# A GRU with routed experts on one core: a wait of VectorE moved to another bank, tanh ahead of z, a reordered head, more expert pieces in the search

## The chip, the cores and the metric

The kernel runs on one core of a Trainium2 chip. The metric is the device time of one execution in microseconds (us), lower is better. The kernel before takes 1180.23 us in the median of 3 runs (1180.09 to 1180.43).

## The reference, cut to what matters

A GRU runs over T = 256 steps of x (16 rows, 256 steps, 512 values); its states are the tokens of a routed layer with 16 experts that share one weight matrix. Each expert takes its 256 best tokens of 4096, and their weighted outputs are added to x.

```
def cell(h, x):
    gi = x @ W_ih + b_ih
    gh = h @ W_hh + b_hh
    i_r, i_z, i_n = jnp.split(gi, 3, axis=-1)
    h_r, h_z, h_n = jnp.split(gh, 3, axis=-1)
    r = jax.nn.sigmoid(i_r + h_r)
    z = jax.nn.sigmoid(i_z + h_z)
    n = jnp.tanh(i_n + r * h_n)
    h_new = (1.0 - z) * n + z * h
...
logits = xf @ router_w + router_b
S = jax.nn.softmax(logits, axis=-1)
G, idx = jax.lax.top_k(S.T, k)          # k = 256
out = jnp.einsum('ekh,hd->ekd', tokens, expert_w) + expert_b
y = jnp.zeros((bs, h)).at[idx.reshape(-1)].add((G[..., None] * out).reshape(-1, h))
return x + y
```

All work is in float32, except for the counts of the search.

## The kernel before, in words

**Stages.** There are four: a head that loads the weights and makes the input products of the first eight steps; the recurrence, 256 steps; the softmax over the experts; and a search for each expert's 256th largest weight, 15 bits of a float one after the other, then the gates, the rest of the expert products and the stores. The order of PE, ACT, DVE, POOL and (in the recurrence) SP is written out by hand: each engine gets its instructions in program order, and a wait on one holds everything behind it on the same engine.

**One step of the recurrence.** The state hs is kept with the 512 values in four blocks of 128 partitions. Each gate has an accumulator bank in PSUM (r, n and z), preset by ACT: r and z with the input products, n with the bias. In each bank the four 128-column blocks of the gate lie in quadrants of 32 partitions. Two steps share a bank: even steps write 16 rows of a quadrant, odd steps 32. A step is

- 96 matmuls on PE (L489, called by h_part): r and n of the first two blocks of hs, r and n of the second two, then z;
- on ACT the sigmoid of r (L579); in even steps the preset of the next r bank (L386) after it;
- on DVE a copy of one element, seen, from r (L583), then t = r * n for two halves (L630) and t + x part for two halves (L632);
- on ACT, for each half, tanh of t (L634) and then the sigmoid of z (L635), and after them presets and copies of the input products (L389, L396, L648 to L651);
- on DVE, by the list of calls, turn_n (L667, a transpose of t), turn_z (L670, of z), less_n (L673, u = h - n), by_z (L678, v = u * z) and plus_n (L681, the new hs), each for the halves 0 and 1. Every plus_n writes half of hs, of which the next step's first matmuls read the first.

In the same steps, after the h matmuls, PE also makes the input products for later steps (x_product, L462: seven products for four steps, in the manner of Strassen, from sums that DVE and ACT keep), router logits (L308) and the expert products of the first ten groups of 8 steps (L371); the number of pieces due is counted in `due`.

**Head.** The queues of SP and ACT carry the loads. Before, SP has the first x block, W_ih's rows 1 and 3 (k = 1, 3), W_hh's gate 2, the second x block (L261), expert weights, router weights, expert bias; ACT has W_ih's k = 0 and 2, W_hh's gates 0 and 1. PE transposes an x block (spread_x, L516), DVE copies it out (L519), PE makes the products of the first eight steps from it (x_part, L403, in four groups by k), and x_done (L414) adds the biases. The second block is transposed after all x_part; `spare` (L546) and `a_sum` (L545) are biases for the input sums, and x_sums makes the operands of the products from the second block. `keep_clock` and `begin_sums` (L90) are matmuls with zeros.

**Softmax and search.** 22 groups are late: their expert products are made from the last steps on, in units. expert_for(n) puts the next n units on PE; a unit is one k of a group for a quarter of the 512 columns (four matmuls of 128 columns, L110, one for each quadrant) until the gates exist, and for all columns after that. When a group is done, ACT copies its bank to ht (L148 to L150) and presets the bank of a following group with the expert bias (late_begin, L132). Four units stand in each of the last two steps, one in last_logits, six ahead of the softmax, five ahead of the search, six in each of its 15 bits, and 14 between the search and the gates. The softmax is the exp on ACT (L353, with a table load ahead of it), sums (L355), reciprocals (L357) and products (L360) on DVE; then PE transposes the weights (L832, L833), they are copied to sT, and each bit is a count on DVE (L760), a matmul that adds counts (L774), and two small operations (L777, L782) that give the next candidate.

Of the kernel before, what the change touches and what calls it, by code (L numbers as in the profile page):

```python
# [13 lines left out]
ALU = mybir.AluOpType  # L14
# [3 lines left out]
def kernel(  # L18
# [15 lines left out]
    nc = tc.nc  # L34
    B, T, D = x.shape
    E = router_w.shape[1]
    P = 128
    QD = 32
    KC = D // P
    TG = P // B  # L40
# [5 lines left out]
    xs = const.tile([P, NG, D], F32, name="xs")  # L46
    ht = const.tile([P, NG, KC, P], F32, name="ht")
    HD = D // 2
    ewr = const.tile([P, KC, E + D], F32, name="ewr")

    lg = const.tile([P, E, NG], F32, name="lg")
    eb = const.tile([P, D], F32, name="eb")
# [51 lines left out]
    ps_m = ctx.enter_context(tc.tile_pool(name="ps_m", bufs=2, space=bass.MemoryType.PSUM))  # L104
# [13 lines left out]
            )  # L118

    whole, halves_d = slice(0, D), [slice(0, HD), slice(HD, D)]  # L120
    quarters = [slice(P * i, P * (i + 1)) for i in range(KC)]

    late_items = [(g, whole) for g in late_groups[:-1]] + [(late_groups[-1], half) for half in halves_d]
    late = []
# [2 lines left out]
    gated = []  # L127

    def late_begin(pool):
        g, cols = late_items[len(late_done) + len(late)]  # L130
        pe = pool.tile([P, D], F32, name="pe", tag="pe")
        nc.scalar.copy(pe[:, cols], eb[:, cols])  # L132
        late.append(pe)

    def late_parts():
        for i, (g, cols) in enumerate(late_items):
            pe = late[0]
            for k in range(KC):

                for part in [cols] if gated or cols != whole else quarters:  # L140
                    late_part(g, pe, k, part)
                    if k == KC - 1 and part.stop == cols.stop:
                        if i + 2 < len(late_items):
                            late_begin(ps_m if (i + 2) % 6 < 2 else late_pool[0])
                        late.pop(0)
                        late_done.append((g, cols))
                        if gated:
                            late_sums[g, cols.start] = pe  # L148
                        else:
                            nc.scalar.copy(wide(g), pe)  # L150
                    yield

    late_pool = []
    parts = late_parts()

    def expert_for(n):
        for _ in range(n):
            next(parts, None)

    with (  # L160
        tc.tile_pool(name="wts", bufs=1) as wts,
# [8 lines left out]
        def slot(s):  # L170
            return 1 + (s - 1) % (2 * TG) if s else 0
# [67 lines left out]
        with tc.manual_schedule(engines={ET.SP, ET.Activation, ET.Pool}):  # L239
            def load_gate(gate, queue):  # L240
                queue.dma_start(
                    out=whh[:, :, gate, :],
                    in_=w_hh[:, gate * D : (gate + 1) * D].rearrange("(c p) n -> p c n", c=KC),
                )

            def load_k(k, queue):
                queue.dma_start(
                    out=wih[:, k].rearrange("p g d -> p (g d)"),
                    in_=w_ih.rearrange("(p c) n -> p c n", c=KC)[:, k, :],
                )  # L250

            nc.gpsimd.dma_start(out=c0, in_=cond)
            nc.sync.dma_start(out=xs[:, 0, :], in_=x[:, 0:TG, :])
            load_k(0, nc.scalar)
            load_k(1, nc.sync)
            load_k(2, nc.scalar)
            load_k(3, nc.sync)
            load_gate(0, nc.scalar)
            load_gate(2, nc.sync)
            load_gate(1, nc.scalar)  # L260
            nc.sync.dma_start(out=xs[:, 1, :], in_=x[:, TG : 2 * TG, :])  # L261
            nc.scalar.activation(dummy, ones[0:1, 0:1], AF.Sigmoid)
            for dst, src in (
                (b_raw[0:1], b_ih.rearrange("(o g d) -> o g d", o=1, d=D)),
                (b_raw[1:2], b_hh.rearrange("(o g d) -> o g d", o=1, d=D)),
                (b_n, b_hh[2 * D :].rearrange("(o d) -> o d", o=1)),
            ):
                nc.gpsimd.dma_start(out=dst, in_=src)
            nc.sync.dma_start(out=ewr[:, :, E:], in_=expert_w.rearrange("(c p) n -> p c n", c=KC))
            nc.sync.dma_start(out=ewr[:, :, 0:E], in_=router_w.rearrange("(c p) n -> p c n", c=KC))  # L270
            nc.gpsimd.dma_start(out=rb, in_=router_b.rearrange("(o e) -> o e", o=1).to_broadcast([P, E]))
            nc.sync.dma_start(out=eb, in_=expert_b.rearrange("(o d) -> o d", o=1).to_broadcast([P, D]))

        def biases(bank):
            for i, rows in enumerate((b_raw[:, 0, :], b_raw[:, 1, :], b_raw[0:1, 2, :], b_n)):
# [225 lines left out]
        def keep_clock(n, banks=idles):  # L501

            for i in range(n):
                begin_sums(banks[i % len(banks)])

        with tc.manual_schedule(engines={ET.PE, ET.Activation, ET.DVE, ET.Pool}):
            make_masks()
            for bank in banks:
                begin_sums(bank)
            keep_clock(8)  # L510
            held = (r_bank, n_bank, z_bank, x_bank0, x_bank1)

            def spread_x(g, bank):
                xT[g] = xtp.tile([P, TG // 2, P], F32, name="xt")
                for c in range(KC):
                    nc.tensor.transpose(bank[:, P * c : P * (c + 1)], xs[:, g, c::KC], ident)  # L516
                for q in range(TG // 2):
                    to = xT[g][:, q, :].rearrange("p (c o b) -> p c o b", c=KC, b=B)
                    nc.vector.tensor_copy(  # L519
                        to, bank.rearrange("p (c b t) -> p c t b", c=KC, t=TG)[:, :, 2 * q : 2 * q + 2, :]  # L520
                    )

            spread_x(0, idles[0])
            keep_clock(2, (idles[1],))
            for k in range(KC):
                for p in range(KC):
                    x_part(p, k, held[p], start=False)
                if k == 1:
                    mixes(0)
                elif k == 3:  # L530
                    for part in range(1, 4):
                        mixes(part)
                if k == 1:
                    for c in range(KC):
                        nc.tensor.transpose(
                            idles[1][:, B * c : B * (c + 1)], c0[:, P * c : P * (c + 1)], ident[0:B, 0:B]
                        )
                    nc.vector.tensor_copy(
                        hs[:, :, 0, :], idles[1][:, 0 : KC * B].rearrange("p (k b) -> p k b", b=B)
                    )  # L540
                elif k == 2:
                    biases(l_bank)
                    nc.vector.tensor_copy(bias, l_bank.rearrange("p (g d) -> p g d", d=P))
            spread_x(1, idles[0])
            nc.scalar.copy(a_sum, bias_f[:, 0:C2])  # L545
            nc.vector.tensor_tensor(spare, bias_f[:, C2 : 2 * C2], bias_f[:, 0:C2], ALU.subtract)  # L546
            for p in range(KC):
                x_done(p, held[p])
                if p == 0:
                    preset_first(0)  # L550
                elif p == 2:
                    preset_rest(0)
            x_sums(1)
            keep_clock(2)

        first, second = range(KC // 2), range(KC // 2, KC)
# [1 line left out]
        with tc.manual_schedule(engines={ET.PE, ET.Activation, ET.DVE, ET.Pool, ET.SP}):  # L558
# [10 lines left out]
            for s in range(T):  # L569
# [10 lines left out]
                if not odd and p < T // 2 - 1:  # L580
                    preset_first(p + 1)

                nc.vector.tensor_copy(seen[0:1, s % 8 : s % 8 + 1], r[0:1, 0:1])  # L583

                late_four = q4 == 0 and 2 < quad <= NQ
                if late_four:
# [45 lines left out]
                    nc.vector.tensor_tensor(t[half], t[half], ring[:, p % AHEAD, 2, cols], ALU.add)  # L632
                for half, cols, ks in halves:
                    nc.scalar.activation(t[half], t[half], AF.Tanh)  # L634
                    nc.scalar.activation(zs[half], zz[p % 2][:, cols], AF.Sigmoid)  # L635
                if not odd and p < T // 2 - 1:
                    preset_rest(p + 1)
# [45 lines left out]
                    )  # L683

                for f, half in (
                    (turn_n, 0), (turn_z, 0), (less_n, 0), (turn_n, 1), (by_z, 0),
                    (turn_z, 1), (plus_n, 0), (less_n, 1), (by_z, 1), (plus_n, 1),
                ):
                    f(half)

# [22 lines left out]
                if s > T - TG:  # L713
                    for g_ in range(RING - 10 + 2 * (c - 1), min(RING, RING - 10 + 2 * c)):
                        nc.gpsimd.tensor_copy(xs[0:1, g_, 0:1], hs[0:1, 0, slot(s), 0:1])
                        nc.sync.dma_start(out=xs[:, g_, :], in_=x[:, g_ * TG : (g_ + 1) * TG, :])
                if s == T - 2:
                    for k in range(KC):
                        gather(NG - 1, k)
# [7 lines left out]
            )  # L727
            for g in range(RING, NG):
                nc.sync.dma_start(out=xs[:, g, :], in_=x[:, g * TG : (g + 1) * TG, :])
            expert_for(6)  # L730
            old, new = slice(0, NG - KC), slice(NG - KC, NG)
            softmax(old, 0)
            less_max(NG // KC - 1, lgt)
# [8 lines left out]
    with (  # L742
# [80 lines left out]
        with tc.manual_schedule(engines={ET.PE, ET.Activation, ET.DVE}):  # L823
# [13 lines left out]

            expert_for(5)
            counts = by_counts(HIGH - LOW + 1)
            top = by_bits(KNOWN, HIGH, LOW, counts, lambda bit: expert_for(6))  # L840

            nc.vector.scalar_tensor_tensor(at_least, sT, top.bitcast(F32), sT, ALU.is_le, ALU.mult)
            most = rt.tile([P, NTOP], F32, name="most")
# [141 lines left out]
```

## Time and profile before

| what | value |
|---|---|
| median of 3 runs | 1180.23 us (1180.09 to 1180.43) |
| profiled execution | 1179.74 us, its span 1177.7 us |
| mean granted TensorE clock | 0.996 |
| PE busy | 1154.3 us (98%) |
| DVE busy | 754.6 us (64%) |
| ACT busy | 548.6 us (47%) |
| POOL busy | 51.8 us (4%) |
| DMA | 37.31 MB, mean 32 GB/s |
| first matmul of the first step | 27.09 us after the span's start |
| load of exp's table | 1087.80 us |
| first count of the search on PE | 1094.71 us |

The span runs from the first to the last instruction. A group's line in the profile reads: line of the kernel, engine, operation, output <- inputs, partitions x elements, how often | busy time in us, mean ns of one | idle time of the engine just before these instructions, and what ended most of it. A line of the timeline has the start in us, the duration, the instruction and how often it follows itself; in brackets the idle time ahead of it and its releaser. The matmuls are pipelined and their ends are modelled, so that a busy PE is not one that lacks slack; starts are sharper than ends. "PEclk" is the clock that the throttle granted, as a share of full speed.

### The profile page before, as it was taken

Reading aid. Unit: us, or ns where it says so; the run is one execution under the profiler, and the core shown is the slowest. Engines: PE = TensorE matmul, PEld = TensorE weight load, DVE = VectorE, ACT = ScalarE, POOL = GpSimd, SP = SyncE. Lnnn points to the kernel's source line nnn. Section 1 sums busy time; section 2 is a strip of 40 time slices with the busy share of each in tenths; the row PEclk is TensorE's granted clock in tenths of the full one; section 3 lists DMA queues with packets and bytes.
Section 4 is the critical chain, followed back from the end, with each engine's and each line's share of the span. In section 5 each row is a group of like instructions: output and inputs, shape, how many; then the busy total and the mean of one; then the engine's idle time right before and its main releaser. Section 6 shows DMA issues by size and latency. Waiting matters only on the chain.

```text
span 1177.7 us, 76649 instructions
## 1 busy us (share of the span) xinstructions
PE 1154.3 (98%) x34125; PEld 994.6 (84%) x34125; DVE 754.6 (64%) x4344; ACT 548.6 (47%) x2343; POOL 51.8 (4%) x218
## 2 busy tenths in 40 slices
PE   7999999999999999999999999999999999999998
PEld 3888888988898888888888888998889889888732
DVE  2566666666666666666667666666666666765762
ACT  0445555444554444545455454555554455544220
POOL 6000000000000000000000000000000000000000
PEclk9999999999999999999999999999999999999999
DMA  8000000000000000000000000000000000003162
GB/s 282 11 13 18 20 20 20 20 21 18 21 22 20 19 20 21 20 19 21 20 16 13 13 11 11 14 11 11 13 13 13 14 13 11 7 4 111 31 215 74
DMA packets 38895, 37.31 MB, mean 32 GB/s; under 512 B 6400, under 2 KB 29712, under 8 KB 38560
## 3 DMA queue, kind: packets, MB, share of 16 engines
q1 hardware_dynamic: 37056, 28.63, 8.4%
q8 instruction: 270, 4.42, 1.5%
q10 hardware_dynamic: 1344, 3.67, 0.9%
q14 instruction: 65, 0.53, 0.1%
q0 software_dynamic: 160, 0.06, 0.1%
HBM read 23.94 MB, written 8.39 MB: 27 GB/s over the span
## 4 chain that ended last, share of the span: by engine, by line
PE 94%; DVE 3%; DMA 2%; ACT 1%; issue 0%; ACTq 0%; DVEq 0%
PE gates L489 61%; PE gates L462 23%; PE pe L110 7%; PE pe L371 3%; DMA xs<-in_x_dram 2%; DVE zT L670 1%; ACT zs L635 0%; DMA wih<-in_L_cond_W_ih_dram 0%; DVE u L673 0%; PE gates L308 0%; DVE nT L667 0%; DVE v L678 0%; DVE hs L681 0%; PE bank L774 0%; DVE xs L546 0%
## 5 line engine op out<-in xcount | busy, mean ns | idle before, releaser
L489 PEld LDWEIGHTS gates<-whh,hs 128*16 128x16 f32 x24576 | 666.9, 103 | 94.9 <-ACT gates L648 27.7
L489 PE MATMUL gates<-whh,hs 128*16 128x128 f32 x24576 | 734.4, 274 | 9.2 <-DVE u L673 5.1
L583 DVE COPY seen<-r 1x1 f32<-1x1 f32 x256 | 36.0, 141 | 252.6 <-ACT r L579 252.6
L579 ACT ACTIVATE r<-gates 128x128 f32<-128x128 f32 x256 | 71.1, 278 | 266.7 <-PE gates L489 266.7
L634 ACT ACTIVATE t<-t 128x64 f32<-128x64 f32 x512 | 129.2, 252 | 137.8 <-DVE t L632 137.8
L667 DVE STREAM_TRANSPOSE nT<-t 128x64 f32<-128x64 f32 x512 | 122.8, 240 | 48.0 <-ACT t L634 48.0
L670 DVE STREAM_TRANSPOSE zT<-zs 128x64 f32<-128x64 f32 x512 | 122.8, 240 | 27.1 <-ACT zs L635 1.3
L635 ACT ACTIVATE zs<-gates 128x64 f32<-128x64 f32 x512 | 112.9, 220 | 32.4 <-PE gates L489 20.3
L462 PE MATMUL gates<-wih,xt 128*32 128x192 f32 x1984 | 111.5, 327 | 0.5 <-issue 0.4
L462 PE MATMUL gates<-xs 128*32 128x192 f32 x1984 | 110.9, 326 | 0.2 <-issue 0.2
L462 PE MATMUL gates<-wih,xs 128*32 128x192 f32 x1984 | 96.2, 326 | 0.0
L678 DVE TENSOR_TENSOR v<-u,zT 128x32 f32<-128x32 f32 x512 | 87.9, 172 | 8.9
L681 DVE TENSOR_TENSOR hs<-v,nT 128x32 f32<-128x32 f32 x512 | 87.4, 171 | 8.7
L630 DVE TENSOR_TENSOR t<-r,gates 128x64 f32<-128x64 f32 x512 | 90.2, 218 | 1.0 <-PE gates L489 1.0
L632 DVE TENSOR_TENSOR t<-t,xs 128x64 f32<-128x64 f32 x512 | 90.6, 218 | 0.0
L673 DVE TENSOR_TENSOR u<-hs,nT 128x32 f32<-128x32 f32 x512 | 84.5, 165 | 0.0
L462 PEld LDWEIGHTS gates<-wih,xt 128*32 128x32 f32 x1984 | 75.3, 110 | 7.3 <-issue 2.3
L110 PE MATMUL pe<-ewr,ht 128*32 128x128 f32 (+2 forms) x1480 | 81.5, 370 | 0.0
L462 PEld LDWEIGHTS gates<-xs 128*32 128x32 f32 x1984 | 76.1, 110 | 5.1 <-issue 1.5
L462 PEld LDWEIGHTS gates<-wih,xs 128*32 128x32 f32 x1984 | 75.7, 110 | 3.7 <-issue 0.5
L110 PEld LDWEIGHTS pe<-ewr,ht 128*32 128x32 f32 x1480 | 42.1, 110 | 32.5 <-issue 30.7
L462 PE MATMUL gates<-xs,xt 128*32 128x192 f32 x992 | 54.1, 326 | 0.0
(129 smaller groups left out, 756.9 us busy)
## 6 DMA issues: line engine op xcount, KB each, us to landing
out_dram<-xs SPq DMA_DIRECT2D x31, 256.0 KB, 3.6
xa<-in_x_dram SPq DMA_DIRECT2D x240, 32.0 KB, 2.9
xs<-in_x_dram SPq DMA_DIRECT2D x17, 256.0 KB, 4.0
xs<-in_x_dram SPq DMA_DIRECT2D x60, 64.0 KB, 3.2
whh<-in_L_cond_W_hh_dram ACTq DMA_DIRECT2D x2, 1024.0 KB, 20.5
wih<-in_L_cond_W_ih_dram ACTq DMA_DIRECT2D x2, 768.0 KB, 6.9
wih<-in_L_cond_W_ih_dram SPq DMA_DIRECT2D x2, 768.0 KB, 11.5
whh<-in_L_cond_W_hh_dram SPq DMA_DIRECT2D x1, 1024.0 KB, 18.9
```

Source lines behind the costliest of these rows:

```text
L110: nc.tensor.matmul(pe[q, cols], ht[:, g, k, q], ewr[:, k, E:][:, cols], start=False, stop=(k == KC - 1), tile_position=(0, QD * j), skip_g ...
L462: nc.tensor.matmul(dst[quadrant(j)], lhs[:, QD * k : QD * (k + 1)], columns(rows[k], j), start=False, stop=(k == 1), tile_position=(0, QD ...
L489: nc.tensor.matmul(dst[quadrant(j, m)], lhs, columns(whh[:, k, gate_, :], j), start=False, stop=(k == KC - 1), tile_position=(0, QD * j), ...
L630: nc.vector.tensor_tensor(t[half], r[:, cols], hn[p % 2][:, cols], ALU.mult)
L632: nc.vector.tensor_tensor(t[half], t[half], ring[:, p % AHEAD, 2, cols], ALU.add)
L634: nc.scalar.activation(t[half], t[half], AF.Tanh)
L635: nc.scalar.activation(zs[half], zz[p % 2][:, cols], AF.Sigmoid)
L667: nc.vector.transpose(nT[half], t[half])
L670: nc.vector.transpose(zT[half], zs[half])
L673: nc.vector.tensor_tensor(u[half], hs[:, halves[half][2], slot(s), :], of_step(nT[half], odd), ALU.subtract)
L678: nc.vector.tensor_tensor(v[half], u[half], of_step(zT[half], odd), ALU.mult)
L681: nc.vector.tensor_tensor(hs[:, halves[half][2], slot(s + 1), :], v[half], of_step(nT[half], odd), ALU.add)
```

## The change

1. In each step, seen is copied from one element of n's bank instead of from r.
2. ACT takes both halves' tanh ahead of both halves' z sigmoid, and DVE's list of calls puts both turn_n first, then less_n 0, turn_z 0, less_n 1, and so on.
3. The loads of the head: both x blocks first, one on each queue; W_ih's and W_hh's parts change queues; expert weights, router weights and expert bias are sent in steps 1 to 5 (the new function load_expert: a one-element POOL copy from hs into the destination, then the transfers on SP), one block of 128 rows a step, the bias in the fifth.
4. In the head, the second x block is transposed right after the first, and a_sum, spare and x_sums of it stand within x_part's loop.
5. A late group is cut in pieces of 256, 128 and 128 columns instead of four quarters. expert_for still counts quarters and keeps in `owed` what a wide piece took too much. 12 units stand ahead of the softmax instead of 6, and 7 in each bit instead of 6. A following group's preset is put after the copy of the finished one, and the rule for which pool its bank comes from differs.

The diff:

```
-    quarters = [slice(P * i, P * (i + 1)) for i in range(KC)]
+    pieces = [slice(0, HD), slice(HD, 3 * P), slice(3 * P, D)]
...
-                for part in [cols] if gated or cols != whole else quarters:
+                for part in [cols] if gated or cols != whole else pieces:
                     late_part(g, pe, k, part)
                     if k == KC - 1 and part.stop == cols.stop:
-                        if i + 2 < len(late_items):
-                            late_begin(ps_m if (i + 2) % 6 < 2 else late_pool[0])
                         late.pop(0)
                         late_done.append((g, cols))
...
+                        if i + 2 < len(late_items):
+                            late_begin(ps_m if i < 1 or (i + 5) % 6 > 3 else late_pool[0])
-                    yield
+                    yield (part.stop - part.start) // P
...
+    owed = [0]
     def expert_for(n):
-        for _ in range(n):
-            next(parts, None)
+        owed[0] += n
+        while owed[0] > 0:
+            owed[0] -= next(parts, owed[0])
...
             nc.sync.dma_start(out=xs[:, 0, :], in_=x[:, 0:TG, :])
-            load_k(0, nc.scalar)
-            load_k(1, nc.sync)
-            load_k(2, nc.scalar)
-            load_k(3, nc.sync)
-            load_gate(0, nc.scalar)
-            load_gate(2, nc.sync)
-            load_gate(1, nc.scalar)
-            nc.sync.dma_start(out=xs[:, 1, :], in_=x[:, TG : 2 * TG, :])
+            nc.scalar.dma_start(out=xs[:, 1, :], in_=x[:, TG : 2 * TG, :])
+            load_k(0, nc.sync)
+            load_k(1, nc.scalar)
+            load_k(2, nc.sync)
+            load_k(3, nc.scalar)
+            load_gate(0, nc.sync)
+            load_gate(2, nc.scalar)
+            load_gate(1, nc.sync)
...
+        def load_expert(part, s):
+            first = eb[0:1, 0:1] if part == KC else ewr[0:1, part, 0:1]
+            nc.gpsimd.tensor_copy(first, hs[0:1, 0, slot(s), 0:1])
+            if part == KC:
+                nc.sync.dma_start(out=eb, in_=expert_b.rearrange("(o d) -> o d", o=1).to_broadcast([P, D]))
+            else:
+                rows = slice(P * part, P * (part + 1))
+                nc.sync.dma_start(out=ewr[:, part, 0:E], in_=router_w[rows, :])
+                nc.sync.dma_start(out=ewr[:, part, E:], in_=expert_w[rows, :])
...
             spread_x(0, idles[0])
+            spread_x(1, idles[1])
             keep_clock(2, (idles[1],))
...
                 elif k == 2:
                     biases(l_bank)
                     nc.vector.tensor_copy(bias, l_bank.rearrange("p (g d) -> p g d", d=P))
-            spread_x(1, idles[0])
-            nc.scalar.copy(a_sum, bias_f[:, 0:C2])
-            nc.vector.tensor_tensor(spare, bias_f[:, C2 : 2 * C2], bias_f[:, 0:C2], ALU.subtract)
+                    nc.scalar.copy(a_sum, bias_f[:, 0:C2])
+                    nc.vector.tensor_tensor(spare, bias_f[:, C2 : 2 * C2], bias_f[:, 0:C2], ALU.subtract)
+                    x_sums(1)
...
-            x_sums(1)
             keep_clock(2)
...
-                nc.vector.tensor_copy(seen[0:1, s % 8 : s % 8 + 1], r[0:1, 0:1])
+                nc.vector.tensor_copy(seen[0:1, s % 8 : s % 8 + 1], hn[p % 2][0:1, 0:1])
...
                 for half, cols, ks in halves:
                     nc.scalar.activation(t[half], t[half], AF.Tanh)
+                for half, cols, ks in halves:
                     nc.scalar.activation(zs[half], zz[p % 2][:, cols], AF.Sigmoid)
...
-                    (turn_n, 0), (turn_z, 0), (less_n, 0), (turn_n, 1), (by_z, 0),
-                    (turn_z, 1), (plus_n, 0), (less_n, 1), (by_z, 1), (plus_n, 1),
+                    (turn_n, 0), (turn_n, 1), (less_n, 0), (turn_z, 0), (less_n, 1),
+                    (by_z, 0), (turn_z, 1), (plus_n, 0), (by_z, 1), (plus_n, 1),
...
+                if 0 < s < KC + 2:
+                    load_expert(s - 1, s)
...
-            expert_for(6)
+            expert_for(12)
...
-            top = by_bits(KNOWN, HIGH, LOW, counts, lambda bit: expert_for(6))
+            top = by_bits(KNOWN, HIGH, LOW, counts, lambda bit: expert_for(7))
```

More of the change, by code (lines that the diff above doesn't have):

```diff
@@ L268 @@
                 nc.gpsimd.dma_start(out=dst, in_=src)
-            nc.sync.dma_start(out=ewr[:, :, E:], in_=expert_w.rearrange("(c p) n -> p c n", c=KC))
-            nc.sync.dma_start(out=ewr[:, :, 0:E], in_=router_w.rearrange("(c p) n -> p c n", c=KC))
             nc.gpsimd.dma_start(out=rb, in_=router_b.rearrange("(o e) -> o e", o=1).to_broadcast([P, E]))
-            nc.sync.dma_start(out=eb, in_=expert_b.rearrange("(o d) -> o d", o=1).to_broadcast([P, D]))
+        def load_expert(part, s):
[7 more added lines that the diff above has]
+                nc.sync.dma_start(out=ewr[:, part, E:], in_=expert_w[rows, :])
         def biases(bank):
```

## The prediction

> **What bounds the kernel now.** I read the chain that ended last and the costliest groups first, then single steps in the timeline, then the two ends of the span. The page alone:
>
> ```profile
> PE 94%; DVE 3%; DMA 2%; ACT 1%; issue 0%; ACTq 0%; DVEq 0%
> ...
> L489 PE MATMUL gates<-whh,hs 128*16 128x128 f32 x24576 | 734.4, 274 | 9.2 <-DVE u L673 5.1
> L583 DVE COPY seen<-r 1x1 f32<-1x1 f32 x256 | 36.0, 141 | 252.6 <-ACT r L579 252.6
> ...
> L630 DVE TENSOR_TENSOR t<-r,gates 128x64 f32<-128x64 f32 x512 | 90.2, 218 | 1.0 <-PE gates L489 1.0
> ```
>
> PE looks like the bound: 94% of the chain, 9 us of idle. The starts of single instructions say otherwise. This is the timeline around the end of one even step:
>
> ```profile
> 504.42 0.28 ACT L579 ACTIVATE r<-gates 128x128 f32<-128x128 f32 x1 [1.13 <-PE gates L489]
> ...
> 504.73 0.14 DVE L583 COPY seen<-r 1x1 f32<-1x1 f32 x1 [1.46 <-ACT r L579]
> 504.86 0.35 DVE L630 TENSOR_TENSOR t<-r,gates 128x64 f32<-128x64 f32 x2
> 505.13 0.35 DVE L632 TENSOR_TENSOR t<-t,xs 128x64 f32<-128x64 f32 x2
> ...
> 505.38 0.26 ACT L634 ACTIVATE t<-t 128x64 f32<-128x64 f32 x1 [0.38 <-DVE t L632]
> ...
> 505.67 0.25 DVE L667 STREAM_TRANSPOSE nT<-t 128x64 f32<-128x64 f32 x1 [0.19 <-ACT t L634]
> ...
> 505.99 0.24 DVE L670 STREAM_TRANSPOSE zT<-zs 128x64 f32<-128x64 f32 x1
> ...
> 506.39 0.15 DVE L678 TENSOR_TENSOR v<-u,zT 128x32 f32<-128x32 f32 x1
> ...
> 506.62 0.15 DVE L681 TENSOR_TENSOR hs<-v,nT 128x32 f32<-128x32 f32 x1
> ...
> 506.91 1.94 PE L489 MATMUL gates<-whh,hs 128*32 128x128 f32 x61
> ```
>
> The first half of hs is written from 506.62, and the next step's first matmul starts 0.29 later. Over all steps that distance is 291 to 298 ns in 98% of 255. So every step ends with a chain r/n -> t -> tanh -> nT, zT -> v -> hs -> PE, and PE's x and expert matmuls fill the gap; what moves that chain moves the step (medians 4.05 us even, 4.12 odd). Counted from a step's first matmul, the median even step has: r starts 1560, seen 1871, PE's count for n rises 1975, t starts 1999, tanh 2520, nT 2810, zT 3128, first hs 3755. **t starts 24 ns after PE's count for n, not when seen is done**: it waits for n anyway. So seen costs the chain nothing today.
>
> **Recurrence, seen.** After the change seen itself waits for n, so it starts where t started, and t comes behind it. The wait that ends last now stands ahead of one more instruction. Price: the issue interval of a one-element operation. Rows: in three steps where DVE came late, so that nothing had to be waited for, t started 28 ns after seen; a one-column operation that had waited was followed after 70 ns; seen to t above, with both waiting, is 130 less what was left of the wait. I take 59 ns (28 to 75). In 121 odd steps the instruction order of the changed kernel has an extra wait instruction on DVE ahead of seen (n's bank has two writers to be waited for, PE and ACT's preset). Rows for one: ACT's ahead of z's sigmoid in odd steps costs 62 ns, DVE's ahead of a later copy 95. Added to the above: 107 ns (90 to 125). Queued behind it on DVE is the whole rest of the step.
>
> **Recurrence, order.** Now nT of both halves stand ahead of zT of the first. Intervals from the rows: transpose to next 159 ns (170 if the first had waited), 128x32 operation to next 70, transpose to dependent 277, operation to dependent 227. Even: nT0 2810, nT1 2980, u0 3139, zT0 3209 (before 3128), u1 3368, v0 3486, h0 after zT1: 3722 (before 3755): 33 ns gained. z's sigmoid of the first half is bound by PE (2871), so the second tanh ahead of it costs nothing. Odd steps, where z0 came 73 ns later and held zT0 back: 3739 against 3827: 88 ns gained. The second half is some 0.2 us earlier, which nobody waits for (PE reads it 0.87 us into the next step). Net: even 59 - 33 = 26 ns lost (5 gained to 42 lost), odd 107 - 88 = 19 lost (2 to 37). 128 x 26 + 121 x 19 = **+5.6 us** (-0.4 to +9.8).
>
> **Head.** The first step starts at 27.09. It waits for the second x block, fifth on SP's queue:
>
> ```profile
> 23.38 0.75 PE L516 MATMUL idle<-ident,xs 128*128 128x128 f32 x4 [1.83 <-DMA xs<-in_x_dram]
> ...
> 26.77 0.27 ACT L386 COPY gates<-xs 128x128 f32<-128x128 f32 x1 [6.79 <-DVE xs L414]
> 27.09 1.00 PEld L489 LDWEIGHTS gates<-whh,hs 128*16 128x16 f32 x24 [1.88 <-ACT gates L386]
> ```
>
> After the change this block comes early, and the end is x_part: four groups of 32 matmuls of 2.79 us, with 1.45 us of transposes, biases and pauses between, 12.6 us (now the last ends at 21.56, after a wait of 1.48). Its start moves from 7.71 to where its first weights land: second on SP instead of first on ACT. The second on SP landed at 11.9. So 11.5 + 12.6 = 24.1, then 0.6 for x_done and preset: first step at 24.7, **2.4 earlier**. The rest: the granted clock.
>
> ```profile
> core 0: us, PE busy (x) PEld busy (x) DVE busy (x) ACT busy (x) POOL busy (x), PEclk, DMA share, GB/s
> 22.55:25.97 3.42, 1.34 (x6) 0.67 (x6) 1.80 (x5) 0.00 (x0) 3.42 (x3) 1.00 0.92 310
> 25.97:32.79 6.82, 5.70 (x104) 4.48 (x108) 4.06 (x16) 1.93 (x9) 0.27 (x2) 0.50 0.06 17
> ```
>
> A stretch with 1.34 us of PE work in 3.42 was followed by 6.82 at clock 0.50, and the first step took 6.56 instead of 4.05: 2.5 lost. With x_part dense up to the first step this goes, but PE now waits earlier, for the weights; if the clock falls there, half of one stretch of 3.41 (1.7) comes back. I take -2.4 - 2.5 + 0.6 for that (one chance in three): **-4.3** (-6.5 to -2). The expert weights go to SP's queue, nine transfers of 8 or 256 KB in steps 1 to 5, each behind a one-element POOL copy. Steps 1 to 5 hold only x transfers on SP, and the first reader (the preset of eb) stands at step 8; cost 0.
>
> **Tail.** Ahead of the softmax 12 units of expert work stand instead of 6. The sixteenth unit, the second of these more, completes a group, so its copy out and the preset of the next are put on ACT **ahead of the table load and exp**. Now:
>
> ```profile
> 1087.80 1.28 ACT L353 ACT_TABLE_LOAD   x1
> ...
> 1089.10 0.58 ACT L353 ACTIVATE lg<-lg 128x448 f32<-128x448 f32 x1
> ...
> 1090.30 0.89 DVE L355 TENSOR_REDUCE tot<-lg 128x28 f32<-128x448 f32 x1
> ...
> 1092.63 0.60 PE L832 MATMUL bank<-ident,lg 128*128 128x128 f32 x3 [2.10 <-DVE lg L360]
> ```
>
> After: PE ends the group near 1090.7 on this time scale, copy 0.59, preset 0.60, load 1.28, exp 0.58 and the reduce at 1093.9 instead of 1090.3: **+3.6** for all that follows, since each next step hangs on the last. PE idles 4.3 us instead of 2.1. The row above had 1.34 busy of 3.42; a gap of 4.3 leaves at most 1.3 of some window of 3.41, so I expect the clock to fall, at the 2.5 of the first step less a fifth: **+2.0** (0 to 2.5). The Trainium skill, page "TensorE: Matmul & The Clock Gate", section on the HAM clock gate, lowers the clock after an idle window of about 3.4 us, free-running; a wholly idle one fits in this gap in one alignment of four, which would make some 0.5 of the 2.0, but the head's row fell with 1.34 us of work in it. The same skill, "ScalarE: Activation LUTs", section What ACT_TABLE_LOAD costs, has 1.38 us of drain behind each load; here exp starts 1.30 after the load's start, so no drain shows, and by the page nothing differs between the two kernels.
>
> More units per bit: 21 quarter units more come before the gates. They would cost 21/4 x 0.858 (the row of a 512-column group) = 4.5 afterwards. A bit takes 1.556 now, PE-bound; seven units in pieces take 0.918 per four, 1.61, with the count 1.71: 15 x 0.16 = +2.4; other units are 0.2 cheaper in all. Net **-2.3**. Tail: 3.6 + 2.0 - 2.3 = **+3.3** (+1.2 to +4.7).
>
> **Sum.** 1179.74 of the profiled execution (span 1177.7 and 2.0 around it) + 5.6 - 4.3 + 3.3 = 1184.3; the median lies 0.5 above that execution: 1184.8, range by the terms 1179 to 1190.5.
>
> **Rivals.** (1) *The wait on n is cheap, and the order wins.* Place: seen to t; it decides at 33 ns in even and 88 in odd steps. For it: the 28 ns of the three steps. Against: these had not waited, and the extra wait instruction. At 28 and 62 (the extra wait alone): 128 x 5 + 121 x 26 = 3.8 gained, total 1180.2 - 3.8 - 4.3 + 3.3 = 1175.4; at no cost at all 15 gained, 1164. Faster. (2) *The softmax isn't delayed*, or ACT catches up: tail -2.3, total 1179.2, the same. Against: ACT works in order. (3) *The head loses its gain*: the first weights land later than 11.9 because both x blocks are ahead, and the clock falls before x_part: 2.0 and 1.7 back, 1188.5. (4) *PE is the bound, as the chain view says*: the recurrence moves nothing, 1179.2. Against: the 295 ns above. That the change doesn't do what it says: only if t waited for n anyway behind seen at no cost, which is (1).
>
> **Chances.** A difference of 0.2% (2.4 us) is what can be told from none. Forecast 0.52; (1) 0.18; (2) 0.12; (3) 0.10; (4) 0.08, a third of it faster. Faster 0.21, same 0.17, slower 0.62. The range takes in (1) at its rows' floor and leaves out its far end.
>
> **What would show it.** In the profile after: seen's releaser is PE, and t starts 50 to 75 ns after seen's start in even steps; first hs to next matmul still 295; steps 4.07 and 4.14. First step at 24 to 25.5 with clock 1.0. Exp near 3.6 later against the last hs, bits of 1.7. I am wrong if the hs write comes earlier in its step than 3755/3827, if the clock holds in the tail, or if x_part starts after 13.

## The result and the profile after

The changed kernel takes 1194.69 us in the median of 4 runs (1192.34 to 1195.68), the kernel before 1180.16 on the same chip (1179.21 to 1180.43): **slower by 1.2%**, ratio 1.0122 with a 95% interval of 1.0104 to 1.0139. The direction was forecast, the size was not: 14.5 us instead of 4.6. The profiled execution took 1193.76 us, its span is 1191.9.

Where the 14.2 us between the two spans lie, from the starts in the two traces:

| stretch | before | after | difference | forecast |
|---|---|---|---|---|
| span's start to the first step | 27.09 | 27.78 | +0.7 | -2.4 and +0.6 |
| first step | 6.56 | 5.68 | -0.9 | -2.5 |
| the other 254 step periods | 1050.6 | 1061.4 | +10.8 | +5.6 |
| last step's first matmul to its last hs write | 4.5 | 4.4 | -0.1 | 0 |
| from there to the first count of the search | 6.0 | 10.2 | +4.2 | +3.6 |
| first count to the end | 83.0 | 82.5 | -0.5 | +2.0 (clock) - 2.3 |

Executions with the steps of the kernel before differ by some 2 us in the third row (1050.6 here, 1053.2 in head_alone, 1049.3 in tail_exp_first), so the medians over the steps further down are the sharper measure.

The page after, with the lines that answer to those of before:

```profile
PE 74%; DVE 20%; ACT 3%; issue 1%; DMA 1%; DVEq 0%; SPq 0%; ACTq 0%
...
L500 PE MATMUL gates<-whh,hs 128*16 128x128 f32 x24576 | 734.3, 273 | 15.3 <-DVE v L690 9.0
L594 DVE COPY seen<-gates 1x1 f32<-1x1 f32 x256 | 37.5, 146 | 327.1 <-PE gates L500 326.8
...
L641 DVE TENSOR_TENSOR t<-r,gates 128x64 f32<-128x64 f32 x512 | 84.3, 200 | 0.0
```

Seen's releaser is now PE, and t never waits: it follows seen. PE's idle time still is only 15 us, so this column never showed what a step waits for; the chain now goes through DVE for 20%. One even step in the timeline (its number is that of the step shown for before):

```profile
508.32 0.15 DVE L594 COPY seen<-gates 1x1 f32<-1x1 f32 x1 [1.77 <-PE gates L500]
508.40 0.33 DVE L641 TENSOR_TENSOR t<-r,gates 128x64 f32<-128x64 f32 x2
...
509.19 0.39 DVE L679 STREAM_TRANSPOSE nT<-t 128x64 f32<-128x64 f32 x2 [0.19 <-ACT t L645]
...
509.58 0.24 DVE L682 STREAM_TRANSPOSE zT<-zs 128x64 f32<-128x64 f32 x1
...
509.85 0.19 DVE L690 TENSOR_TENSOR v<-u,zT 128x32 f32<-128x32 f32 x1
509.96 0.24 DVE L682 STREAM_TRANSPOSE zT<-zs 128x64 f32<-128x64 f32 x1
...
510.12 0.15 DVE L693 TENSOR_TENSOR hs<-v,nT 128x32 f32<-128x32 f32 x1
...
510.42 1.85 PE L500 MATMUL gates<-whh,hs 128*32 128x128 f32 x57
```

From the step's first matmul (506.32) to the first write of hs are 3.80 us, where before had 3.76; from that write to the next matmul 0.30 (before 0.29). (The prediction's 98% is too high: in the kernel before, this distance lies between 291 and 298 ns in 91% of the 255 steps, and in the others PE comes up to 0.3 us later.) From the end of the write to the next matmul are 146 ns in the median, before and after. Over all steps (medians, ns after the step's first matmul; t0, nT0, zT0 and v0 are the first half's t, turn_n, turn_z and by_z):

| even steps | t0 | nT0 | zT0 | v0 | first hs | next step |
|---|---|---|---|---|---|---|
| before | 1999 | 2810 | 3128 | 3527 | 3755 | 4051 |
| after | 2074 | 2864 | 3253 | 3525 | 3795 | 4092 |

In odd steps the first hs comes at 3877 instead of 3827 and the period is 4172 instead of 4122. 128 x 41 + 121 x 50 = 11.3 (121 odd steps have the extra wait), about the 10.8 of the table.

### The profile page after: what moved, and what is told of

It is laid out like the page before. It is cut to its first block, busy times and chain, and to the rows that moved or that the text cites. A ratio compares the mean times of both kernels' runs of the same rounds, so it can differ in the third digit from the quotient of the medians.

```text
span 1191.9 us, 76486 instructions
## 1 busy us (share of the span) xinstructions
PE 1160.7 (97%) x33973; PEld 993.5 (83%) x33973; DVE 717.7 (60%) x4344; ACT 524.2 (44%) x2345; POOL 52.4 (4%) x223
## 4 chain that ended last, share of the span: by engine, by line
PE 74%; DVE 20%; ACT 3%; issue 1%; DMA 1%; DVEq 0%; SPq 0%; ACTq 0%
PE gates L500 51%; PE gates L473 12%; PE pe L110 6%; DVE nT L679 4%; DVE v L690 3%; DVE zT L682 3%; ACT t L645 3%; DVE t L641 3%; PE pe L382 2%; DVE u L685 2%; DVE seen L594 2%; DVE t L643 2%; DMA wih<-in_L_cond_W_ih_dram 1%; PE gates L414 1%; DVE hs L693 1%
## 5 line engine op out<-in xcount | busy, mean ns | idle before, releaser
L594 DVE COPY seen<-gates 1x1 f32<-1x1 f32 x256 | 37.5, 146 | 327.1 <-PE gates L500 326.8
L645 ACT ACTIVATE t<-t 128x64 f32<-128x64 f32 x512 | 103.2, 249 | 159.3 <-DVE t L643 159.3
L679 DVE STREAM_TRANSPOSE nT<-t 128x64 f32<-128x64 f32 x512 | 100.3, 234 | 48.0 <-ACT t L645 47.9
L690 DVE TENSOR_TENSOR v<-u,zT 128x32 f32<-128x32 f32 x512 | 98.6, 193 | 0.0
L643 DVE TENSOR_TENSOR t<-t,xs 128x64 f32<-128x64 f32 x512 | 87.6, 206 | 0.1
L641 DVE TENSOR_TENSOR t<-r,gates 128x64 f32<-128x64 f32 x512 | 84.3, 200 | 0.0
L647 ACT ACTIVATE zs<-gates 128x64 f32<-128x64 f32 x512 | 83.1, 213 | 0.6 <-PE gates L500 0.4
L110 PE MATMUL pe<-ewr,ht 128*32 128x128 f32 (+2 forms) x1328 | 82.5, 399 | 0.0
L685 DVE TENSOR_TENSOR u<-hs,nT 128x32 f32<-128x32 f32 x512 | 78.3, 153 | 0.0
## 6 DMA issues: line engine op xcount, KB each, us to landing
wih<-in_L_cond_W_ih_dram ACTq DMA_DIRECT2D x2, 768.0 KB, 10.6
wih<-in_L_cond_W_ih_dram SPq DMA_DIRECT2D x2, 768.0 KB, 11.5
```

The costliest lines, as they stand in the source:

```text
L110: nc.tensor.matmul(pe[q, cols], ht[:, g, k, q], ewr[:, k, E:][:, cols], start=False, stop=(k == KC - 1), tile_position=(0, QD * j), skip_g ...
L641: nc.vector.tensor_tensor(t[half], r[:, cols], hn[p % 2][:, cols], ALU.mult)
L679: nc.vector.transpose(nT[half], t[half])
L685: nc.vector.tensor_tensor(u[half], hs[:, halves[half][2], slot(s), :], of_step(nT[half], odd), ALU.subtract)
L690: nc.vector.tensor_tensor(v[half], u[half], of_step(zT[half], odd), ALU.mult)
```

## The experiments

Each run is compared with runs of the kernel before on its own chip: the ratio stands with its 95% interval. Code lines are those of the kernel that the run starts from.

### The recurrence: the wait alone, the order alone

**seen_alone**, the kernel before with one line of the change:

```
-nc.vector.tensor_copy(seen[0:1, s % 8 : s % 8 + 1], r[0:1, 0:1])
+nc.vector.tensor_copy(seen[0:1, s % 8 : s % 8 + 1], hn[p % 2][0:1, 0:1])
```

> The kernel before with the first edit alone: seen is copied from n's bank, all else as before. Theory (the edits interact): in the order of before, the first half's chain is held by z, not by t: zT of the first half starts 257 ns after z's sigmoid (even 2871 to 3128, odd 2944 to 3201), while nT of the first half would let it start at 2810 + 159 = 2969 in even and 2823 + 159 = 2982 in odd steps. A wait of 75 ns (even) or 144 ns (odd), as the changed kernel's trace has it, fits into these 159 and 219 ns: 1180 us, within 1.5 us. Rival (the wait is on the chain whatever the order): 75 x 128 + 144 x 121 = 27 us more, 1207 us.

Measured: 1179.30 against 1180.30, ratio 0.9993 (0.9983 to 1.0002): no difference. t0 is as late as in the changed kernel (2074 and 2156), nT0 too (2863 and 2945), but zT0 stands at 3127 and 3201, where it was, and the periods are 4050 and 4122. One even step:

```profile
505.24 0.15 DVE L583 COPY seen<-gates 1x1 f32<-1x1 f32 x1 [1.71 <-PE gates L489]
...
506.10 0.24 DVE L667 STREAM_TRANSPOSE nT<-t 128x64 f32<-128x64 f32 x1 [0.19 <-ACT t L634]
506.11 0.22 ACT L635 ACTIVATE zs<-gates 128x64 f32<-128x64 f32 x1
...
506.37 0.25 DVE L670 STREAM_TRANSPOSE zT<-zs 128x64 f32<-128x64 f32 x1
```

zT follows z's sigmoid by 0.26, and nT by 0.27, where one transpose needs only 0.16 to the next: in the old order the first half waits for z, and the late t hides in that.

**order_alone**, the kernel before with the tanh edit and the changed list of calls, seen from r:

> The kernel before with the second edit alone: both tanh ahead of z's sigmoids and the changed list of calls on DVE; seen from r as before. Theory: without the wait the changed order writes the first half of hs at 3795 - 75 = 3720 instead of 3755 in even steps and at 3877 - 144 = 3733 instead of 3827 in odd ones: 35 x 128 + 94 x 121 = 16 us less, 1164 us, with 295 ns from that write to the next step's first matmul still. Rival (PE is the bound, as its 94% of the chain says): 1180 us and a longer distance from the write to the matmul. Rival (the order itself costs): more than 1180.

Measured: 1169.29 against 1180.30, ratio 0.9910 (0.9894 to 0.9927). The order gains 11 us, not 16: first hs at 3741 and 3753, so 14 and 74 ns earlier than before (14 x 128 + 74 x 121 = 10.7). The distance to the next matmul stays at 295 to 297: PE is not the bound.

**after_seen_r**, the changed kernel with seen from r again:

> The changed kernel with the first edit undone: seen from r again. Theory: the wait of 75 ns in even and 144 ns in odd steps goes wholly, since in the changed order nothing hides it: 75 x 128 + 144 x 121 = 27 us less than the changed kernel's 1194.7: 1167.7 us. Rival (PE becomes the bound as soon as a step is shorter than before's): no less than the 1184 that undoing the recurrence's loss of 10.7 gives.

Measured: 1172.42 against 1180.30, ratio 0.9933 (0.9915 to 0.9950), 22.3 us less than the changed kernel. nT0 comes 54 ns earlier in even steps (2810 for 2864) and 122 in odd ones (2822 for 2944): 54 x 128 + 122 x 121 = 21.7. I had taken the 75 and 144 ns by which t0 moved; some 20 of them come back before nT0, since t to tanh takes 500 ns where it took 521 (one operation of t lasts 200 ns for 218 in the page's lines).

**after_seen_even**, the changed kernel with seen from n's bank in even steps alone:

```
-... hn[p % 2][0:1, 0:1])
+... (r if odd else hn[p % 2])[0:1, 0:1])
```

> The changed kernel with seen from n's bank in even steps only, from r in odd ones. Theory (in odd steps the wait costs 122 ns, of which about 70 are the extra wait instruction for ACT's preset of the bank, in even ones 54): 122 x 121 = 14.8 us less than 1194.7, 1179.9 us. Rival (both parities pay alike, 85 ns): 10.5 less, 1184.2 us.

Measured: 1179.03 against 1178.98, ratio 0.9993 (0.9981 to 1.0004), 15.7 less than the changed kernel's 1194.69 (15.2 by the two ratios, since the chips differ), as the dearer odd steps demand and not as equal prices would have it. In the changed kernel seen starts 23 ns after PE's count for n (the semaphore that tells that n's matmuls are done) in even steps and 93 in odd ones: the extra wait instruction is 70 of the 122 ns.

**order_z1_late**, the kernel before with seen from r, both tanh first and a list of my own:

```
(turn_n, 0), (turn_n, 1),
# even: (turn_z, 0), (less_n, 0), (less_n, 1)
# odd:  (less_n, 0), (turn_z, 0), (less_n, 1)
(by_z, 0), (plus_n, 0), (turn_z, 1), (by_z, 1), (plus_n, 1),
```

> The kernel before with seen from r, both tanh first, and another list of calls: turn_z of the second half behind plus_n of the first, and in even steps turn_z of the first half ahead of less_n. Theory (the step is set by DVE's chain to the first half of hs): in even steps that write comes 77 ns ahead of where the changed list alone puts it (3741 to 3664), in odd steps 44 (3753 to 3709): 15 us less than 1169.3, 1154 us, with 295 ns from the write to the next matmul. Rival (PE has no more slack: 94% of the chain): 1165 to 1169 us and a longer distance from the write to the matmul.

Measured: 1170.86 against 1178.98, ratio 0.9925 (0.9902 to 0.9947), no better than the changed list. The theory fell in this form, and not to PE. The first hs starts at 3708 and 3710, but the next matmul comes 338 ns after it, not 295: a plus_n directly behind the by_z on which it hangs starts earlier and lasts longer (192 ns for the first half, 150 in order_alone), and in sum (3708 + 338 = 4046, 3741 + 295 = 4036) nothing is won. The longer distance was the rival's sign for PE, but from the end of the write to the matmul are 146 ns, as in the other kernels: PE still comes when the write is through. The transpose between the two stands in time that plus_n would wait anyway. And in even steps the earlier zT0 (3128) made u0 late (3298 for 3124), on which v0 hangs just as much.

### The head

**head_alone**, the head's edits and the later sending of the expert weights:

> The kernel before with the head's edits and the later sending of the expert weights alone. Theory from the changed kernel's trace: the first step starts 0.7 later and is 0.9 shorter, and the transfers in steps 1 to 5 cost nothing: 1180.0 us, within 1.5. Rival (the head's gain of 4.3 that was forecast is there and was taken back by something else): 1176. Rival (the transfers hold up the first steps): over 1182.

Measured: 1181.27 against 1180.30, ratio 1.0007 (0.9997 to 1.0017). The gain that was forecast isn't there, and the steps with the expert transfers have their usual periods but for one: the sixth took 4450 ns instead of 4121, since ACT began z's sigmoid 0.33 us late. head_x_done_first shows the same, the changed kernel doesn't; the cause is open. Its head is that of the changed kernel, whose trace shows what took the gain. Engine by engine (PE, then DVE, ACT, POOL):

```profile
11.67 6.89 PE L414 MATMUL gates<-wih,xt 128*32 128x384 f32 x64 [2.90 <-DMA wih<-in_L_cond_W_ih_dram]
...
22.56 2.79 PE L414 MATMUL gates<-wih,xt 128*32 128x384 f32 x32
```

```profile
23.45 2.57 DVE L557 TENSOR_TENSOR xs<-bias 128x192 f32<-128x192 f32 x1
...
26.87 1.94 DVE L425 TENSOR_TENSOR xs<-gates,bias 128x384 f32<-128x384 f32 x4
```

```profile
22.35 3.45 POOL L441 TENSOR_TENSOR wih<-wih 128x1536 f32<-128x1536 f32 x1
```

x_part started at 11.67, where the forecast had 11.5, but its first two groups took 6.89 us instead of 2 x 2.79: the granted clock is 0.64 in the mean from 12.3 to 15.7 (0.50 from 11.38 to 14.79), and it fell there in all five profiles with this order of loads. x_part is through at 25.35, and x_done, which adds its biases, starts only at 26.87. Ahead of it on DVE stand spare (L557), which lasts until POOL's last subtraction ends (22.35 + 3.45 = 25.80; spare 26.02), and the four x_sums. Before, spare ended at 26.20, with POOL's subtraction at 25.99: there too POOL held the first step up, by some 0.9 us (spare took 1.23 instead of 0.35), on top of the second x block.

**head_x_done_first**, the head alone with two pieces moved:

```
 # in x_part's loop, k == 2
-nc.vector.tensor_tensor(spare, ...)
-x_sums(1)
...
 # behind the loop with x_done
+nc.vector.tensor_tensor(spare, ...)
+x_sums(1)
```

> The head's edits alone, but with spare and x_sums behind x_done on DVE instead of ahead of it. In the changed head spare (DVE, 128x192) takes 2.46 us and ends at 25.82, as POOL's last subtraction does (25.80), and x_done follows only after x_sums. Theory (the operations put ahead of x_done are what the first step waits for): x_done starts near 25.4 when x_part is through, the first step at 25.9 instead of 27.6: 1179.6 us, where the head's edits alone gave 1181.3. Rival (POOL holds x_done up in the same way as spare): x_done is long too and the first step starts at 26.4 or later.

Measured: 1177.84 against 1180.12, ratio 0.9981 (0.9972 to 0.9991). The first step starts at 25.40. x_done is not held by POOL: each of its four operations takes 0.56 us (0.55 in the changed kernel, with POOL idle) and starts within 0.11 us of the end of the block of x_part that it adds. So they run beside x_part's last group, which the operations ahead of them had kept them from: from the end of x_part to the first step are 0.47 us, in head_alone 2.32.

**head_k0_first**, that with the loads' order changed:

```
 # SP:  x block 0, k 1, k 3, gate 2
 # ACT: k 0, k 2, x block 1, gate 0, gate 1
 # spread_x(1) at k == 2 of x_part's loop
```

> As the run with x_done first, and the weights of x_part's first group first on ACT's queue again, the second x block third there, its transposes in x_part's loop. Theory (x_part started 4 us late because its weights stood second): x_part starts at 7.7 and ends near 22.4, the first step starts near 23: 1180.2 - 4.1 = 1176 us, and up to 2.5 less if the clock holds. Rival (POOL's four subtractions, which end near 26, hold x_done): first step at 26.4, 1179.5 us.

Measured: 1177.19 against 1180.12, ratio 0.9976 (0.9966 to 0.9986), between the theory's 1176 and the rival's 1179.5. The first step starts at 22.67, as the theory had it, and then lasts 6.32 us: spare stands ahead of seen on DVE, starts at 22.74, and lasts 3.48 us, until POOL is through. Against head_x_done_first 2.7 us were earned and 2.3 given back within one step.

### The tail

**tail_alone**, the tail's edits:

> The kernel before with the tail's edits alone (pieces, 12 units ahead of the softmax, 7 in each bit). Theory from the changed kernel's trace: table load and exp stand behind the copy and preset of the finished group and come 3.6 us later against the last hs; PE's gap ahead of the transposes goes from 2.1 to 4.2 us; from the first count to the end 0.5 to 1.2 less: 1183.2 us, within 1.5. Rival (the search gains what was forecast, 2.3, and the clock holds): 1181.5.

Measured: 1182.87 against 1178.98, ratio 1.0028 (1.0018 to 1.0038). The changed kernel's ACT, and then PE, behind its last step (last hs write at 1099.19):

```profile
1101.24 0.59 ACT L148 COPY ht<-pe 128x512 f32<-128x512 f32 x1 [2.97 <-PE pe L110]
1101.86 0.59 ACT L132 COPY pe<-eb 128x512 f32<-128x512 f32 x1
1102.47 1.28 ACT L364 ACT_TABLE_LOAD   x1
1103.76 0.72 ACT L364 ACTIVATE lg<-lg 128x448 f32<-128x448 f32 x2
...
1106.72 0.70 PE L846 MATMUL bank<-ident,lg 128*128 128x128 f32 x3 [4.21 <-DVE lg L371]
```

ACT waits 2.97 us for PE to finish the group, though it could have loaded the table; copy and preset take 1.2 more. From the last hs write to the transposes are 7.53 us where before had 3.93: the 3.6 that was forecast; in tail_alone's own trace they are 7.38. Then the clock fell, as forecast (the columns are those of the prediction's rows; PEclk is the third from the end):

```profile
1103.90:1107.30 3.40, 0.58 (x4) 0.56 (x4) 2.13 (x6) 0.58 (x2) 0.00 (x0) 0.96 0.00 0
1107.30:1110.70 3.40, 3.40 (x51) 2.07 (x53) 2.03 (x7) 0.48 (x1) 0.00 (x0) 0.53 0.00 0
```

**tail_exp_first**, the tail's edits with the twelve units written behind the exps:

```
-expert_for(12)
 ...
 softmax(old, 1)
 softmax(new, 0)
+expert_for(12)
```

> The tail's edits alone, with the 12 units written behind both exps instead of ahead of them: PE's order is the same, but on ACT the table load and the exps come ahead of the copy and the preset. Theory (ACT's order is the cause): the 3.6 us go, 1179.5 us, and exp starts 0.4 us after the last hs again. Rival (PE's six further units delay the softmax, or the pieces cost more than they save): like the tail's edits alone, 1183.

Measured: 1177.26 against 1178.98, ratio 0.9984 (0.9974 to 0.9995), now faster than before. Its ACT:

```profile
1085.18 1.28 ACT L356 ACT_TABLE_LOAD   x1
1086.47 0.58 ACT L356 ACTIVATE lg<-lg 128x448 f32<-128x448 f32 x1
1087.96 0.26 ACT L356 ACTIVATE lg<-lg 128x64 f32<-128x64 f32 x1 [0.91 <-DVE lg L345]
1088.12 0.58 ACT L148 COPY ht<-pe 128x512 f32<-128x512 f32 x1
```

The same units stand on PE in the same order; only ACT's program order differs, and exp starts 0.39 us behind the last hs write again. PE's gap ahead of the transposes is 0.88 us, and the clock holds at 1.00.

### The parts that gained, together

**best**, the order with seen from r, head_k0_first and tail_exp_first:

> All that gained: the changed order of tanh and calls with seen from r, the tail's edits with the units behind the exps, the head as in the run with x_part's first weights first. Theory (the parts add up): 1180.2 - 10.6 - 1.9 - 4 = 1163.5 us. Rival (the head gains nothing): 1167.5. Rival (parts eat each other up): over 1169.

Measured: 1166.08 against 1180.12, ratio 0.9877 (0.9861 to 0.9894). Its first step lasts 6.48 us, for the reason seen above, here with POOL's subtraction beside spare:

```profile
22.85 3.48 DVE L563 TENSOR_TENSOR xs<-bias 128x192 f32<-128x192 f32 x1
...
22.66 3.46 POOL L441 TENSOR_TENSOR wih<-wih 128x1536 f32<-128x1536 f32 x1
```

PE idled meanwhile, the clock fell to 0.50 at 30.26, and the second step took 5.64 us instead of 4.05. The profiled execution is the slowest of the four (1169.16).

**best_late_spare**, that with spare, x_sums and the copy of spare behind the first step's list of calls:

```
     f(half)
+if s == 0:
+    nc.vector.tensor_tensor(spare, ...)
+    x_sums(1)
+    nc.scalar.copy(e_sum, spare)
```

> As the run of all parts that gained, with spare, x_sums and the copy of spare moved behind the first step's list of calls. There the first step started at 22.8 but spare, which starts on DVE at 22.85, lasted 3.48 us, to 0.2 behind the end of POOL's last subtraction, and seen and t of the first step stood behind it: that step took 6.48 us. Theory (DVE's spare waits for POOL's subtraction, and what is behind it on DVE too): the first step takes 4.05 us and the time is 2.4 less, 1163.7 us. Rival (the first step is long for another reason, the clock or the weights): no change, 1166.

Measured: 1163.06 against 1180.00, ratio 0.9854 (0.9838 to 0.9871): **1.5% faster than the kernel before** and the fastest of all. The first step takes 4.98 us, not 4.05. What is left of the wait moved to the next operation with two inputs from SBUF:

```profile
24.11 0.35 DVE L639 TENSOR_TENSOR t<-r,gates 128x64 f32<-128x64 f32 x2
24.37 1.28 DVE L641 TENSOR_TENSOR t<-t,xs 128x64 f32<-128x64 f32 x2
```

The first, which reads one input from PSUM, takes its usual 0.35 for both halves; the second, usually 0.35 too, takes 1.28 and ends at 25.65, 0.21 after POOL's subtraction. The clock holds, and the second step takes 4.05, which fits the 3.0 us gained instead of 2.4.

**The sum of the parts.** By the ratios, the order alone gave -10.6 us, the wait in the new order +22.3, the head +0.8 and the tail +3.3: 15.8, where the whole change has 14.4. Each ratio is known to 1 or 2 us, so nothing large is missing.

## Why the prediction was wrong, point by point

Between the two profiled spans lie 9.6 us more than forecast: 5.2 in the recurrence, 4.1 in the head and 0.3 in the tail. None of the three signs named for being wrong came: hs wasn't written earlier, the clock fell in the tail, and x_part started at 11.67. The bounds of the three terms, added up, reach from 1174.5 to 1192.7; the stated range is narrower, and the measured time lies above both.

- **The step is set by DVE's chain, not by PE: right.** From the first hs write to the next matmul the median is 295 to 297 ns in the changed kernel and in order_alone, as before; the order alone moved the time although PE fills 94% of the chain view.
- **"t waits for n anyway", and so seen, put behind that wait, delays t: right.** The price at nT0 was 54 ns in even steps (59 forecast) and 122 in odd ones (107 forecast). The even price is close partly by luck: t itself moved by 75, and some 20 came back in t's own operations. The odd one was added up too low: the rows had 62 to 95 for the extra wait (70 measured), and 59 + 62 is 121 already; seen to t took 76 in both parities.
- **The order's gain was mis-sized:** 33 and 88 ns forecast, 14 and 74 measured by order_alone. The step that failed is "operation to next 70": by_z has to wait for zT, and after an operation that has waited the next starts 110 ns later (v0 3470, zT1 3580), not 70. In even steps half of these 40 were made up (v0 came 16 ns earlier than forecast). With the wait: 54 - 14 = 40 and 122 - 74 = 48 ns lost, against 26 and 19 forecast. That is 10.9 us instead of 5.6, a little past the upper bound of 9.8; the order makes 4.1 of the 5.3 us missed.
- **"Then 0.6 for x_done and preset" failed.** It left out spare and x_sums, which the change put ahead of x_done on DVE: from the end of x_part to the first step are 2.43 us instead of 0.6, and with the two moved behind x_done 0.47. The fall of the clock in x_part, held at one chance in three, came in all five profiles and cost 1.3. So the first step came 0.7 later instead of 2.4 earlier. The 2.5 of the slow first step came back only in part (0.9) in this profile, and that was chance: with the same head the clock fell in the first step in two of four profiles (5.7 to 5.8 us here and in after_seen_even, 4.1 in head_alone and after_seen_r), and with the head of before that step took 5.3 to 6.6. "It waits for the second x block" was right in the main, but POOL's subtraction held spare, and so x_done, another 0.9.
- **The expert weights in steps 1 to 5 cost nothing: right** in the changed kernel; two other profiles have 0.33 us in one step.
- **The tail was right in its main term, and two other terms were off and cancelled.** 3.6 forecast and measured. The clock fell, but cost some 1.1 us and not 2.0: from the transposes to the first count are 2.71 us and the first bit takes 2.42, where tail_exp_first, whose clock holds, has 2.02 and 1.97. The search and what is behind it saved some 1.0 instead of 2.3 (bits of 1.55 to 1.98, 1.75 in the mean behind the first, 1.71 forecast). So +3.7 against +3.3 is partly luck.
- **Rivals.** (1), the cheap wait, fell: it cost 54 and 122 ns, and in the order as it really gained (14 and 74, not 33 and 88) anything above these loses. (2) and (4) fell as argued. (3) came true in its outcome and only partly in its reasons: the weights landed in time, the clock fell (1.3), and DVE's order cost the rest.

## What to carry to other kernels

A wait that ends last is free where something later holds the same chain: the moved wait cost nothing in the old order and 22 us in the new one, and the new order gained 11 us without it. So try the parts of a change alone, and ask of each what its neighbour hides. On an engine that works in program order, whatever is written ahead of the critical operation counts, even if it belongs to other work: a copy that waits for PE, and a preset, ahead of the exp cost 3.6 us, and writing the same calls a few lines later took that away.

## What the runs showed that I had not expected

- **A DVE operation with two inputs from SBUF waits for POOL's subtraction.** spare (128x192, both inputs in SBUF) takes 0.35 us with POOL idle (best_late_spare). In the other 13 profiles it starts beside POOL's last subtraction (3.42 to 3.48 us), lasts 0.36 to 3.48 us, and ends 0.21 to 0.22 us after it every time. x_done, with one input in PSUM, took 0.56 for 0.55 beside the same subtraction. The Trainium skill, "GPSIMD Engine Reference", section Specifications, says that GpSimd's SBUF interfaces are shared with VectorE and that there is contention with instructions that have two SBUF inputs; the runs agree and give the size: not a slowdown but a wait for POOL's end.
- **PE's clock falls without a wholly idle stretch.** In every trace the changes of the clock lie on a grid of 3.41 us. In the 14 profiles a clock of 1.00 fell behind each stretch of that grid with up to 1.34 us of PE work and held behind each with 1.6 or more; between 1.42 and 1.53 both occur (PE's ends are modelled, so these are rough). In the kernel before it fell after 1.34 us of work with no pause longer than 0.97 (22.55 to 25.97). That also settles the softmax: with PE's gap of 2.1 us the clock fell in four profiles (1.31 us of work in the stretch) and held in three (1.70 to 1.92), by where the grid lay; with 4.2 it fell in all four, with 0.9 it held in all three.
